# A message-passing layer in one stream of matmuls: the source-row products stand two tiles later, layer two three tiles later

## The chip, the cores and the metric

The kernel runs on one core of one Trainium2 chip. The metric is the device time of one execution in microseconds (us), the median of several runs. A core has five engines that run their own instruction streams and wait for each other by semaphores: TensorE (PE; its weight loads are shown as PEld), VectorE (DVE), ScalarE (ACT), GpSimd (POOL) and SyncE (SP, which here only issues DMAs).

## The reference

One layer of a graph network with 12500 nodes, 400000 edges sorted by `dst`, 32 features, 64 hidden units:

```python
h = jnp.maximum(_layernorm(x, axis=-1), 0.0)
# _L0_gnn_ref(h, edge_index = [src, dst], edge_attr_32, W1, b1, W2, b2):
e_feat = jnp.concatenate([h[src], h[dst], edge_attr], axis=-1)   # 400000 x 96
hid = jax.nn.relu(e_feat @ W1 + b1)
v = hid @ W2 + b2                                                # 400000 x 32
x_cand = jax.ops.segment_max(v, dst, num_segments=num_nodes)
out = x + jnp.maximum(x_cand, h)
```

## The kernel before

**Tiling.** The edges are cut into 4 stripes (`NS`), and each stripe into 196 chunks (`NCH`) of 512 edges (`C`). Four stripes of a chunk lie side by side on the 128 partitions, 32 features each. The main loop takes two chunks at a time: `for c in range(0, NCH - 4, 2)`, with `a, b = c + 2, c + 3` as the pair of chunks that the *next* iteration will need. So one iteration, called a pair below, finishes chunks c and c+1 and prepares rows for a and b. There are 98 pairs in all.

**Layer one** of a pair fills four PSUM banks `ph` (one per stripe) in three steps, 8 matmuls each: `edges_into` adds the products with the edge features (tile `ea`), `windows_into` those with the destination nodes (spans: `of` is a one-hot matrix that ACT makes, `qf` a window of already multiplied rows `q_d`), and `rows_into` those with the source rows (tile `ht`). A matmul of these steps shows as two in the profile, 16 per step. Then `relu` (ACT) makes `hid`, `second_layer` multiplies by W2 into two banks `pv`, and DVE's `scan` runs a running maximum along the sorted edges (a penalty `pb` starts a new segment). `fewest` picks the segment ends, `add_b2` (ACT) makes `sb`, and in the next pair `leave_1` transposes it on PE, `leave_2` places it with the one-hot `last`, ACT copies to `wo`, and `leave_3` adds and writes rows to `top_d` by DMAs of SP.

**Source rows** come in two ways. Twelve of sixteen groups of 128 rows per chunk are gathered by POOL (`gather`: one indirect DMA per group into tile `gh`). The other four groups per chunk, and one more in 76 of the chunks (`MMX`), are picked on PE: `tile(c, m)` multiplies one-hot matrices `hot` (DVE makes four of seven slices in `one_hots`, ACT three in `one_hots_act`) by the node table `hs`, 14 matmuls of 128x448 into one bank `pv`, and DVE multiplies by a `mask` and takes a maximum (`one`, `gm`). This is called a tile. `to_features(c, part)` transposes gathered or picked rows into `ht` (DVE); the last part, `J`, turns the picked rows.

**What sets the order.** The kernel is written under a manual schedule: each engine executes its instructions in the order in which the Python code calls them, and only the waits are added. PSUM banks `ph`, `pv` come from one ring of 7 (`bank`). POOL's gathers are paced by hand: the table `HELD` maps the position of a gather within a pair to an instruction (by pair distance and name, such as `(2, 'ea')`) that must have passed first; `passes(...)` marks these.

Of the kernel before, what the change touches and what calls it, by code (L numbers as in the profile page):

```python
# [36 lines left out]
J = C // P  # L37
# [30 lines left out]
LATE = NCH - 8  # L68
END = LATE - 16
PIECE = 2 * A0  # L70
GP = 3
HELD = {0: (3, 'b1'), 1: (3, 'b1 max'), 2: (3, 'b2'), 3: (3, 'b2 max'), 4: (3, 'b3'), 5: (3, 'b3 max'), 6: (3, 'n0'),
        8: (2, 'ea'), 9: (2, 'ht'), 10: (2, 'tr'), 12: (2, 'relu'), 13: (2, 'a1'), 14: (2, 'a1 max'), 15: (2, 'a2'),
        16: (2, 'a2 max'), 17: (2, 'a3'), 19: (2, 'lv'), 20: (2, 'scan'), 21: (2, 'b0'), 22: (2, 'b0 max')}
# [16 lines left out]
def gnn_kernel(ctx, tc, x, src, src_mm, src_x, src_t, dst, dst_end, dst_ext, lo, lo_c, ends_b, edge_attr, weights, w1, w2, b2, out):  # L91
# [501 lines left out]
    with tc.tile_pool(name="edges", bufs=3) as pool, tc.tile_pool(name="edges_ps", bufs=1, space=PSUM) as ps:  # L593
# [106 lines left out]
        def leave_1(c, sb):  # L700

            px = bank("pv")[:, :P]
            passes(c // 2 + 1, "tr", nc.tensor.transpose(px, sb, ident))  # L703
# [235 lines left out]
        for c in range(0, NCH - 4, 2):  # L939
            a, b = c + 2, c + 3  # L940
            if c:
                ph = edges_into(c)
                windows_into(c, ph)
            rows_into(c, ph)
            if c % LOAD:
                load_edges(c + LOAD // 2 + AHEAD)
# [7 lines left out]
            if c == LATE + 2:  # L954
                ea = pool.tile([P, LOAD * C], F32, name="ea", bufs=2)
                rows_of(1, slice(32, 64), [ea[:, :LOAD * C // 2], ea[:, LOAD * C // 2:]])
                for k in range(c, NCH, 2):
                    late_loads(k)
            if c:
                so = leave_1(c - 2, sb)  # L960
                one_hots(b, 0, 2)
                one_hots_act(b)
                one_hots(b, 2, by_act(b).start)
                mask_of(b)
                if c == LATE + 2:
                    finish(0)
                tile(a, 1)
                to_features(a, 1)
                leave_rest(so)
                one_hot_x(b)  # L970
                tile(a, 2)
                to_features(a, 2)
                last_next = lasts(c)
                tile(a, 3)
            else:
                tile(b, 3)
                tile(a + 2, 0)
            pv = second_layer(c, hid)
# [29 lines left out]
            if not c:  # L1008
                last_next = lasts(c)
# [80 lines left out]
        c = NCH - 4  # L1090
# [198 lines left out]
```

## Time and profile before

| | |
|---|---|
| median of 3 runs | 3555.01 us (3553.36 to 3557.04) |
| profiled execution, its own time | 3587.46 us |
| span of the profiled execution | 3585.7 us |
| mean granted TensorE clock | 0.939 |
| busy: PE, PEld | 3293.3 us (92%), 2511.2 us (70%) |
| busy: DVE, ACT, POOL | 2437.4 us (68%), 1402.3 us (39%), 2161.2 us (60%) |
| matmuls | 18468 |

The profile is one execution, so 1.8 us lie outside its span, and it is 0.9% longer than the median of the runs. Busy PE means that a matmul was in flight; its ends are modelled, and it says little of how dense the matmuls stand. The start times of successive groups in the timeline tell more. "issue" as the releaser of a wait means that the profile shows nothing that the engine waited for.

### The profile page before, as it was taken

How to read it: one execution, taken by the hardware profiler on the slowest of the kernel's cores; microseconds unless marked ns; L12 is line 12 of the kernel's file. 1: busy time of each engine (PE TensorE's matmuls, PEld its weight loads, DVE VectorE, ACT ScalarE, POOL GpSimd, SP SyncE). 2: the span in 40 equal slices, each digit the busy share in tenths (PEclk: the TensorE clock that was granted, in tenths of full speed). 3: DMA queues.
4: the chain of work that ended last, by engine and by line, in shares of the span. 5: the costliest groups of instructions: out<-in, count | busy, mean ns of one | idle time of the engine just before them, and what ended most of it. 6: DMA issues, size and time to landing. Idle time of an engine off the chain costs nothing.

```text
span 3585.7 us, 55025 instructions
## 1 busy us (share of the span) xinstructions
PE 3293.3 (92%) x18468; PEld 2511.2 (70%) x18468; DVE 2437.4 (68%) x4987; ACT 1402.3 (39%) x2276; POOL 2161.2 (60%) x2295
## 2 busy tenths in 40 slices
PE   5788999999999999999999999999999999999996
PEld 3466767776767677767776767777767777677773
DVE  6467667767677677676666666767666766666765
ACT  4233434343443333434333334333333344343342
POOL 6665666665666666656666666666666666666562
PEclk8799999999999999999999999999999999999997
DMA  5322222222222222222222222222222222221222
GB/s 188 82 60 58 58 59 58 71 50 58 68 63 52 58 65 63 52 58 62 62 56 64 62 59 56 59 63 66 50 63 63 62 53 62 61 66 50 59 58 64
DMA packets 183894, 227.88 MB, mean 64 GB/s; under 512 B 115365, under 2 KB 155445, under 8 KB 170806
## 3 DMA queue, kind: packets, MB, share of 16 engines
q10 hardware_dynamic: 36228, 109.11, 9.6%
q0 software_dynamic: 72992, 37.52, 7.7%
q1 hardware_dynamic: 74386, 77.71, 7.0%
q8 instruction: 145, 2.38, 0.3%
q14 instruction: 143, 1.17, 0.1%
HBM read 212.63 MB, written 11.47 MB: 63 GB/s over the span
## 4 chain that ended last, share of the span: by engine, by line
PE 70%; DVE 12%; issue 8%; another core or an unknown queue 4%; DMA 1%; ACT 1%; POOL 1%; SPq 1%; DVEq 0%; ACTq 0%; POOLq 0%
PE pv L351 53%; PE ph L837 12%; DVE one L358 3%; PE pv L871 3%; DVE hot L311 2%; DVE pv L878 2%; DVE ht L375 1%; PE pv L727 1%; POOL gh L186 1%; DVE sm L885 1%; PE pv L703 1%; DMA top_d<-wo 1%; DVE gm L359 1%; DVE m L892 0%
## 5 line engine op out<-in xcount | busy, mean ns | idle before, releaser
L186 POOL DMA_INDIRECT gh<-h_d,src_i x2249 | 2123.6, 944 | 1355.9 <-issue 511.8
L351 PE MATMUL pv<-hs,hot 128*128 128x448 f32 x10752 | 2369.3, 378 | 112.5 <-issue 76.7
L351 PEld LDWEIGHTS pv<-hs,hot 128*128 128x128 f32 x10752 | 2096.1, 197 | 326.8 <-issue 127.0
L358 DVE TENSOR_TENSOR one<-pv,mask 128x448 f32<-128x448 f32 x768 | 470.4, 612 | 982.7 <-issue 340.1
L862 ACT ACTIVATE hid<-ph,wt 128x512 f32<-128x512 f32 x392 | 244.2, 687 | 982.0 <-remote 491.2
L359 DVE TENSOR_REDUCE gm<-one 128x32 f32<-128x448 f32 x768 | 476.3, 620 | 26.4
L311 DVE TENSOR_TENSOR hot<-kb,consts 128x1024 fp32r<-128x1024 f16 (+1 forms) x379 | 445.4, 1194 | 0.0
L837 PE MATMUL ph<-ht,wt 32*64 32x512 f32 x1568 | 350.4, 696 | 95.0 <-issue 59.3
L325 ACT ACTIVATE hot<-away,ones 128x512 fp32r<-128x512 f32 x582 | 421.8, 725 | 36.9 <-remote 17.9
L324 ACT ACTIVATE away<-kb,key_n 128x512 f32<-128x512 f16 x582 | 415.7, 714 | 0.0
L718 ACT ACTIVATE wo<-pv 128x256 f32<-128x256 f32 x95 | 36.5, 384 | 689.7 <-remote 383.9
L837 PEld LDWEIGHTS ph<-ht,wt 32*64 32x64 f32 x1568 | 84.1, 141 | 294.3 <-issue 246.2
L878 DVE TENSOR_TENSOR_SCAN pv<-pb,kept,pv 128x512 f32<-128x512 bf16 x193 | 244.0, 1264 | 15.1 <-remote 15.0
L375 DVE STREAM_TRANSPOSE ht<-gh 128x96 f32<-128x96 f32 x774 | 207.9, 269 | 2.6
L697 ACT ACTIVATE sb<-m,wt 128x128 f32<-128x128 f32 x97 | 39.1, 403 | 423.1 <-DVE sm L885 239.4
L351 PE MATMUL pv<-hs,xg 128*128 128x448 f32 x760 | 169.2, 366 | 8.1 <-issue 8.1
L351 PEld LDWEIGHTS pv<-hs,xg 128*128 128x128 f32 x760 | 143.1, 189 | 21.4 <-issue 11.6
L837 PE MATMUL ph<-of,qf 32*64 32x512 f32 x1552 | 136.3, 606 | 14.3 <-ACT of L672 11.2
L672 ACT ACTIVATE of<-of,ones 128x512 f32<-128x512 f32 x194 | 140.6, 725 | 6.3
L892 DVE TENSOR_REDUCE m<-sm 128x64 f32<-128x512 f32 x194 | 133.1, 686 | 6.7
L671 ACT ACTIVATE of<-db,below 128x512 f32<-128x512 int32 x194 | 137.4, 708 | 0.0
L837 PE MATMUL ph<-ea,wt 32*64 32x512 f32 x1568 | 131.3, 619 | 3.7 <-issue 2.6
(139 smaller groups left out, 1309.4 us busy)
## 6 DMA issues: line engine op xcount, KB each, us to landing
ea<-in_edge_attr SPq DMA_DIRECT2D x49, 1024.0 KB
db<-in_dst_ext ACTq DMA_DIRECT2D x48, 1024.0 KB
gh<-h_d,src_i POOLq DMA_INDIRECT x2249
pb<-pen_d ACTq DMA_DIRECT2D x47, 512.5 KB
kb<-key_d ACTq DMA_DIRECT2D x47, 512.0 KB
top_d<-wo SPq DMA_DIRECT2D x752, 3.0 KB
qf<-q_d SPq DMA_DIRECT2D x392, 16.0 KB
q_d<-qs SPq DMA_DIRECT2D x6, 512.0 KB
```

Of the source, the lines that this page charges most:

```text
L186: ins = nc.gpsimd.indirect_dma_start(out=parts[-1][:, i, :], out_offset=None, in_=h_d[:, :], in_offset=bass.IndirectOffsetOnAxis(ap=src_i[ ...
L311: nc.vector.tensor_tensor(hot_of(c)[:, start:stop], keys[c][:, None, :].to_broadcast([P, n, MM * P]), key_ps[:, start:stop, None].to_broad ...
L324: nc.scalar.activation(away, keys[c], AF.Square, bias=key_n[:, k:k + 1])
L325: nc.scalar.activation(hot_of(c)[:, k], away, AF.Relu, bias=ones, scale=-1.0)
L351: ins = nc.tensor.matmul(po, hot[k], hs[:, part, k].rearrange("p f a -> p (f a)"), start=(k == 0 and part == 0), stop=(k == A1 - 1 and par ...
L358: nc.vector.tensor_tensor(one, of_group, mask[:, None, :].to_broadcast([P, D, A0]), op=ALU.mult)
L359: passes(c // 2 - 1, "ab"[c % 2] + str(m) + " max", nc.vector.tensor_reduce(row, one, axis=AX.X, op=ALU.max))
L375: nc.vector.transpose(ht[:, r].rearrange("p k e -> p (k e)"), gh[c][part][:, :r.stop - r.start].rearrange("p k f -> p (k f)"))
L672: nc.scalar.activation(of, of, AF.Relu, bias=ones, scale=-1.0)
L837: ins = nc.tensor.matmul(ph[s][x * HID:(x + 1) * HID], w[g], e[g], start=start, stop=stop)
L862: passes(c // 2, "relu", nc.scalar.activation(hid[k], of, AF.Relu, bias=b1c))
L878: ins = nc.vector.tensor_tensor_scan(pv, pen[:, :C], pv, -LOW if before is None else before, op0=ALU.add, op1=ALU.max)
```

## The change

No instruction is added or removed from the work; two or three waits apart, each engine has the same instructions in another order.

- After `edges_into` and `windows_into`, tiles (a,1) and (a,2) now come before `rows_into` and `relu`; tile (a,3) and the transpose of `leave_1` follow.
- `second_layer` and `leave_2` now stand behind tiles (a,3), (b,0) and (b,1), where they stood behind (a,1), (a,2) and (a,3).
- DVE's one-hots, masks and row transposes and ACT's one-hots for chunk a+2 move with the tiles that they belong to; `one_hots(b, ...)` now stands ahead of `relu`.
- `HELD` is written anew: which gather waits for which instruction.

```diff
-HELD = {0: (3, 'b1'), 1: (3, 'b1 max'), 2: (3, 'b2'), 3: (3, 'b2 max'), 4: (3, 'b3'), 5: (3, 'b3 max'), 6: (3, 'n0'),
...
+HELD = {0: (3, 'b2'), 2: (3, 'b2 max'), 3: (3, 'b3'), 4: (3, 'b3 max'), 7: (3, 'n0'),
...
             if c:
                 ph = edges_into(c)
                 windows_into(c, ph)
+                one_hots(b, 0, 2)
+                one_hots_act(b)
+                tile(a, 1)
+                to_features(a, 1)
+                one_hots(b, 2, by_act(b).start)
+                mask_of(b)
...
+                tile(a, 2)
+                to_features(a, 2)
             rows_into(c, ph)
...
             hid = relu(c)
...
             if c:
+                tile(a, 3)
                 so = leave_1(c - 2, sb)
-                one_hots(b, 0, 2)
-                one_hots_act(b)
-                one_hots(b, 2, by_act(b).start)
-                mask_of(b)
...
-                tile(a, 1)
-                to_features(a, 1)
+                to_features(a, 3)
+                to_features(a, J)
+                one_hot_x(b)
+                tile(b, 0)
+                to_features(b, 0)
                 leave_rest(so)
-                one_hot_x(b)
-                tile(a, 2)
-                to_features(a, 2)
+                one_hots(a + 2, 0, 2)
+                one_hots_act(a + 2)
+                tile(b, 1)
+                to_features(b, 1)
                 last_next = lasts(c)
-                tile(a, 3)
+                one_hots(a + 2, 2, by_act(a + 2).start)
+                mask_of(a + 2)
...
             pv = second_layer(c, hid)
             if c:
                 pw = leave_2(c - 2, so, last)
-            if c:
-                one_hots_act(a + 2)
...
-            if c:
-                to_features(a, 3)
-                to_features(a, J)
...
-            if c:
-                one_hots(a + 2, 0, 2)
             found, kept = scan(c, pv[0], kept)
             m8 = fewest(found, 0)
             if c:
-                tile(b, 0)
-                to_features(b, 0)
+                tile(b, 2)
+                to_features(b, 2)
             found, kept = scan(c + 1, pv[1], kept)
             sb = add_b2(fewest(found, 1, m8))
...
-            if c:
-                tile(b, 1)
-            to_features(b, 1)
...
-            if c:
-                one_hots(a + 2, 2, by_act(a + 2).start)
-                mask_of(a + 2)
             last = last_next
-            if c:
-                tile(b, 2)
-            to_features(b, 2)
```

TensorE, one pair in the steady state before (`ea`, `of`, `ht` are the three steps of layer one, `x14` of `pv<-hs,hot` is one tile, `zero` and `xg` hold the one-hots of the extra group, `ident,sb` is the transpose of `leave_1`, `hid,wt` layer two, `so,last` `leave_2`):

```order
L837 MATMUL ph<-ea,wt 64x512 x8
L837 MATMUL ph<-of,qf 64x512 x8
L837 MATMUL ph<-ht,wt 64x512 x8
L703 MATMUL pv<-ident,sb 128x128
L351 MATMUL pv<-hs,hot 128x448 x42
L871 MATMUL pv<-hid,wt 32x512 x8
L727 MATMUL pv<-so,last 128x256 x2
L351 MATMUL pv<-hs,hot 128x448 x56
```

The same pair of the changed kernel, on TensorE:

```order
L837 MATMUL ph<-ea,wt 64x512 x8
L837 MATMUL ph<-of,qf 64x512 x8
L351 MATMUL pv<-hs,hot 128x448 x28
L837 MATMUL ph<-ht,wt 64x512 x8
L351 MATMUL pv<-hs,hot 128x448 x14
L703 MATMUL pv<-ident,sb 128x128
L351 MATMUL pv<-hs,hot 128x448 x28
L871 MATMUL pv<-hid,wt 32x512 x8
L727 MATMUL pv<-so,last 128x256 x2
```

The 24 small matmuls of layer one no longer stand in one row: 16 of them, then two tiles, then the other 8. After `leave_2` follow 42 to 56 large matmuls where 70 to 84 followed.

VectorE, around layer two's scan before (`pv<-pb,kept,pv` is the scan, `one` and `gm` evaluate a tile, `hot` is a one-hot slice pair for a tile of the next pair):

```order
L378 STREAM_TRANSPOSE ht<-gm 128x128
L311 TENSOR_TENSOR hot<-kb,consts 128x1024
L878 SCALAR_TENSOR_TENSOR pv<-pb,kept,pv 128x512
L883 COPY kept<-pv 128x1
L885 SCALAR_TENSOR_TENSOR sm<-pb,pv 128x512
```

The same place of the changed kernel, on VectorE:

```order
L358 TENSOR_TENSOR one<-pv,mask 128x448
L359 TENSOR_REDUCE gm<-one 128x32
L375 STREAM_TRANSPOSE ht<-gh 128x96
L681 TENSOR_TENSOR last<-consts,at 128x256
L311 TENSOR_TENSOR hot<-kb,consts 128x1024
L330 TENSOR_TENSOR mask<-consts,place_k 128x56
L878 SCALAR_TENSOR_TENSOR pv<-pb,kept,pv 128x512
```

Ahead of the scan now stand a tile's evaluation (of (b,1)), the one-hot `last`, a `hot` slice pair and a mask, which stood elsewhere in the pair.

On ScalarE the six activations of `one_hots_act(b)` now stand between the spans' one-hots and `relu`, where they stood behind `relu`; the DMAs that load `db` and `pb` are issued behind them.

More of the change, by code (lines that the diff above doesn't have):

```diff
@@ L71 @@
 GP = 3
-HELD = {0: (3, 'b1'), 1: (3, 'b1 max'), 2: (3, 'b2'), 3: (3, 'b2 max'), 4: (3, 'b3'), 5: (3, 'b3 max'), 6: (3, 'n0'),
-        8: (2, 'ea'), 9: (2, 'ht'), 10: (2, 'tr'), 12: (2, 'relu'), 13: (2, 'a1'), 14: (2, 'a1 max'), 15: (2, 'a2'),
-        16: (2, 'a2 max'), 17: (2, 'a3'), 19: (2, 'lv'), 20: (2, 'scan'), 21: (2, 'b0'), 22: (2, 'b0 max')}
+HELD = {0: (3, 'b2'), 2: (3, 'b2 max'), 3: (3, 'b3'), 4: (3, 'b3 max'), 7: (3, 'n0'),
+        8: (2, 'ea'), 11: (2, 'a1'), 12: (2, 'a1 max'), 13: (2, 'a2'), 14: (2, 'ht'), 15: (2, 'a2 max'), 16: (2, 'relu'),
+        17: (2, 'a3'), 19: (2, 'b0'), 20: (2, 'b0 max'), 21: (2, 'b1'), 22: (2, 'lv'), 23: (2, 'scan')}
 BANKS = 7
@@ L943, in gnn_kernel @@
                 windows_into(c, ph)
+                one_hots(b, 0, 2)
[4 more added lines that the diff above has]
+                mask_of(b)
+                if c == LATE + 2:
+                    finish(0)
+                tile(a, 2)
+                to_features(a, 2)
             rows_into(c, ph)
@@ L1004, in gnn_kernel @@
                 finish(2)
-            if c:
-                tile(b, 1)
-            to_features(b, 1)
             if not c:
+                to_features(b, 1)
                 last_next = lasts(c)
-            if c:
-                one_hots(a + 2, 2, by_act(a + 2).start)
-                mask_of(a + 2)
+                to_features(b, 2)
             last = last_next
-            if c:
-                tile(b, 2)
-            to_features(b, 2)
             if c == LATE + 2:
```

2 lines of the change are left out of this document (removed).

## The prediction

> **What bounds the kernel now.** I read the engines' shares and the chain of waits first, then the costliest groups, then TensorE's timeline of single pairs, and last the clock.
>
> ```profile
> PE 3293.3 (92%) x18468; PEld 2511.2 (70%) x18468; DVE 2437.4 (68%) x4987; ACT 1402.3 (39%) x2276; POOL 2161.2 (60%) x2295
> PEclk8799999999999999999999999999999999999997
> PE 70%; DVE 12%; issue 8%; another core or an unknown queue 4%; DMA 1%; ACT 1%; POOL 1%; SPq 1%; DVEq 0%; ACTq 0%; POOLq 0%
> ```
>
> TensorE carries 70% of the chain and is in flight 92% of the span, so the question is how much of that is matmul at full pace. Layer one's three steps have the same count and nearly the same shapes, and should cost the same:
>
> ```profile
> L837 PE MATMUL ph<-ht,wt 32*64 32x512 f32 x1568 | 350.4, 696 | 95.0 <-issue 59.3
> L837 PE MATMUL ph<-of,qf 32*64 32x512 f32 x1552 | 136.3, 606 | 14.3 <-ACT of L672 11.2
> ```
>
> They don't: with the idle time ahead of it, the step with source rows takes 445.4 us and the one with spans 150.6. The timeline of one pair shows where (start, length, matmuls):
>
> ```profile
> 1674.77 1.11 PE L837 MATMUL ph<-ea,wt 32*64 32x512 f32 x16
> 1675.68 1.06 PE L837 MATMUL ph<-of,qf 32*64 32x512 f32 x16
> 1676.54 1.92 PE L837 MATMUL ph<-ht,wt 32*64 32x512 f32 x8
> 1678.80 1.36 PE L837 MATMUL ph<-ht,wt 32*64 32x512 f32 x3 [0.34 <-issue]
> 1680.32 3.38 PE L837 MATMUL ph<-ht,wt 32*64 32x512 f32 x5 [0.17 <-issue]
> 1683.63 0.47 PE L703 MATMUL pv<-ident,sb 128*128 128x128 f32 x1
> 1683.76 10.83 PE L351 MATMUL pv<-hs,hot 128*128 128x448 f32 x42
> 1694.52 1.09 PE L871 MATMUL pv<-hid,wt 64*32 64x512 f32 x16
> ...
> 1695.88 11.38 PE L351 MATMUL pv<-hs,hot 128*128 128x448 f32 x56
> ...
> 1712.78 0.69 PE L837 MATMUL ph<-ea,wt 32*64 32x512 f32 x8
> ```
>
> Edge and span products take 0.91 and 0.86 us from start to start, the source rows 7.09 us (1676.54 to 1683.63). VectorE is not what they wait for: the last transpose into `ht` was over at 1675.51, before the first of them.
>
> ```profile
> 1675.24 0.27 DVE L378 STREAM_TRANSPOSE ht<-gm 128x128 f32<-128x128 f32 x1
> 1930.69 0.27 DVE L378 STREAM_TRANSPOSE ht<-gm 128x128 f32<-128x128 f32 x1
> ```
>
> The second row belongs to another pair, where that transpose was late and TensorE had to wait for it until 1930.96, 0.84 us. There the rest came at once:
>
> ```profile
> 1930.12 0.59 PE L837 MATMUL ph<-ht,wt 32*64 32x512 f32 x1
> ...
> 1930.55 1.58 PE L837 MATMUL ph<-ht,wt 32*64 32x512 f32 x15
> 1932.06 0.33 PE L703 MATMUL pv<-ident,sb 128*128 128x128 f32 x1
> 1932.14 8.65 PE L351 MATMUL pv<-hs,hot 128*128 128x448 f32 x42
> 1940.73 1.09 PE L871 MATMUL pv<-hid,wt 64*32 64x512 f32 x16
> ...
> 1942.09 0.97 PE L351 MATMUL pv<-hs,hot 128*128 128x448 f32 x4
> ...
> 1945.39 9.80 PE L351 MATMUL pv<-hs,hot 128*128 128x448 f32 x48 [1.04 <-issue]
> ...
> 1960.78 0.69 PE L837 MATMUL ph<-ea,wt 32*64 32x512 f32 x8
> ```
>
> All sixteen pass in 1.94 us with the wait. So a wait of under a microsecond removes a stall of six. My reading: after 32 small matmuls in a row TensorE has used up the instructions that were ready, the next ones arrive one or two at a time, and a short wait, or slower large matmuls, lets them catch up. In this pair the shortage shows later and smaller, behind layer two's 16 small ones: the 84 matmuls from 1942.09 take 18.69 us, where those from 1695.88 took 16.90 (0.2 each).
>
> The stall has a second price, the clock:
>
> ```profile
> core 0: 3585.7 us, clock 0.939
> 1674.80:1683.60 8.80, 8.17 (x49) 1.97 (x48) 4.38 (x9) 0.91 (x2) 4.91 (x6) 0.89 0.41 82
> 1683.60:1712.80 29.20, 29.20 (x149) 25.84 (x149) 21.02 (x44) 13.27 (x22) 18.43 (x20) 0.92 0.24 65
> 1928.09:1960.78 32.69, 31.45 (x194) 25.03 (x193) 24.34 (x50) 14.30 (x23) 19.60 (x21) 1.00 0.20 50
> ```
>
> (Column eight is the granted clock.) The pair with the long stall runs at 0.92 behind it, and its first three tiles take 10.76 us instead of 8.59; the pair without runs at 1.00. The first takes 38.0 us, the second 32.7.
>
> [...]
>
> **The change, part by part.** The sum is made against 3587.5 us, the profiled execution's own time; the median of the runs is 3555.0, or 0.991 of it.
>
> ```profile
> L862 ACT ACTIVATE hid<-ph,wt x392: 676/687/702, 104.7 to 3567.6; 128x512 f32<-128x512 f32 x196
> ```
>
> 392 activations of four per pair are 98 pairs, so a pair takes (3567.6 - 104.7) / 97 = 35.7 us on average.
>
> *Source rows behind two tiles.* Edges and spans are then 32 small matmuls in a row, not 48, and 28 large ones (2 x 14 at 0.2 us, 5.7 us) pass before the next 16. Sixteen behind large ones are what layer two is now, and its row runs in 1.02 us. I take the source rows at the spans' price: 445.4 - 150.6 x 1568/1552 = 293 us gone.
>
> *The clock.* (1 - 0.939) x 3585.7 = 219 us of full clock are lost. The first two slices and the last stand at 8, 7 and 7 tenths; I estimate 60 us for them. Of the other 159, 70% lie behind the stall (0.08 x 29.2 = 2.3 us against 0.11 x 8.8 = 1.0 inside it, which is already counted): 111 us gone.
>
> *The shortage comes back smaller.* 32 small matmuls, now followed by tile (a,1), stand between the 16 of layer two, with 1.79 us behind them, and the 48 now, with 6. At least nothing, at most those 6 us a pair (582 in all). I take 1.8 us, since what follows is a large tile as there, in the pairs that had the long stall and hence had not this one: at 38.0 us for a long pair and 32.7 for a short one, an average of 35.7 makes 55 of 97 long, so 99 us come back. The short pairs' waits for the late transpose go, 42 x 0.84 = 35 us, since two tiles now cover it. One-hots are made earlier too, and of the 36 us that tiles waited for something named I count off 25, an estimate from the first row:
>
> ```profile
> L351 PE MATMUL pv<-hs,hot 128*128 128x448 f32 x10752 | 2369.3, 378 | 112.5 <-issue 76.7
> L186 POOL DMA_INDIRECT gh<-h_d,src_i x2249 | 2123.6, 944 | 1355.9 <-issue 511.8
> ```
>
> *Layer two later.* Behind its end now stand `leave_2` and three or four tiles instead of five or six: 0.34 + 4 x 14 x 0.2 + 0.9 = 12.5 us until the next pair's span products, 9.6 without the extra group. In that time VectorE must scan twice and ScalarE make the spans' one-hots. Prices from before, start to start:
>
> ```profile
> 1591.05 1.28 DVE L878 TENSOR_TENSOR_SCAN pv<-pb,kept,pv 128x512 f32<-128x512 bf16 x1
> ...
> 1593.76 0.61 DVE L358 TENSOR_TENSOR one<-pv,mask 128x448 f32<-128x448 f32 x1
> ...
> 1595.13 1.25 DVE L878 TENSOR_TENSOR_SCAN pv<-pb,kept,pv 128x512 f32<-128x512 bf16 x1
> ...
> 1597.81 0.41 DVE L764 TENSOR_TENSOR wo<-pv,wo 128x256 f32<-128x256 f32 x1
> 1597.92 0.40 ACT L697 ACTIVATE sb<-m,wt 128x128 f32<-128x128 f32 x1 [4.85 <-DVE sm L885]
> ...
> 1600.35 0.72 ACT L672 ACTIVATE of<-of,ones 128x512 f32<-128x512 f32 x1
> ```
>
> and, of the costliest groups:
>
> ```profile
> L311 DVE TENSOR_TENSOR hot<-kb,consts 128x1024 fp32r<-128x1024 f16 x377 | 440.9, 1188 | 0.0
> L681 DVE TENSOR_TENSOR last<-consts,at 128x256 fp32r<-128x256 f32 x96 | 37.0, 385 | 0.0
> ```
>
> Scan 2.71, a tile 1.37, scan 2.68, then 3.2 for `sb` and four activations: 10.0 us. Ahead of them VectorE has tile (b,1), 1.37 us, `last`, 0.39, and a `hot` pair, 1.19: 3 us from that tile's end, 2 of them behind layer two's end. So 12 us against 12.5: hidden in the 76 pairs with an extra group, by half a microsecond, and 2.4 us late in the other 18 of the steady state: 43 us. What waits behind is the span products and the whole of TensorE.
>
> *Banks, DMAs, gathers.* The four `ph` banks are held for two tiles longer; the ring still hands out each bank seven allocations later, and the next users (transpose, (b,0), (b,1), layer two) stand behind `relu`, so nothing. `db`, `pb` and keys are issued up to 4.3 us later (six activations), two pairs ahead of use: nothing. A gather takes 0.944 us and 0.30 to the next; 2249 over 97 pairs are 23.2 x 1.245 = 28.9 us a pair, with the holds some 30. That cover ends if TensorE gets below 30 us.
>
> The sum: 3587 - 293 - 111 + 99 - 35 - 25 + 43 = 3265, or 3.3 us less a pair. From the other side, the short pair of 32.7 less its wait is 31.8; with 30 in the 21 pairs without the group that is 31.4 on average, and 3587 - 97 x 4.3 = 3170. I take the middle, 3218; by 0.991, **3190 us**. Its own range goes from all shortage gone, with gathers the bound (3587 - 97 x 5.5 = 3054, or 3025), to 33.3 a pair (3355, or 3325).
>
> **The rivals.**
>
> *The same stall, elsewhere.* If TensorE runs dry after 32 small matmuls as after 48, tile (a,1) stalls by 6 us. Only clock, transposes and one-hots are won, and the late spans lost: 3587 - 111 - 35 - 25 + 43 = 3459, or 3430. For it: the shortage did move, to 1943. Against: there it was 1.8.
>
> *The stall travels.* If it belongs to the products with source rows themselves, they stall wherever they stand, 6 us between two tiles, and the clock still falls: no change, 3555. The pair at 1930 speaks against it. [...]
>
> *Spans too late, slower.* If VectorE comes to layer two's scan with a backlog, span products wait in every pair and give the shortage no cover that counts. The gain is (293 + 111 - 99 + 35 + 25) / 97 = 3.8 us a pair, so it decides once they wait that long in each; at 5 us a pair, 3265 - 43 + 97 x 5 = 3707, or 3675. VectorE is busy 68%, 25 of 35.7 us, which leaves room; the chain has none.
>
> *Another bound first.* Gathers and holds at 34 us a pair: 3587 - 97 x 1.7 = 3422, or 3390.
>
> **How the numbers follow.** Forecast 0.64, same stall elsewhere 0.12, another bound 0.10, stall travels 0.05, slower by late spans 0.09. The predicted time is the forecast's. The range runs from 3030 to 3430, which takes in the first three. Within 0.2% is about what a measurement of this kernel can tell from no change. Faster 0.86, same 0.05, slower 0.09.
>
> **What would show it.** The group of source-row products falls from 350 busy and 95 idle to the spans' 136 and 14; the granted clock rises from 0.939 to above 0.97; tile (a,1) begins with gaps of "issue". Idle time before the span products, released by ScalarE, would show the late chain. I am wrong if the source-row group keeps its time, or if TensorE's tiles wait longer than these products did.

## The result: 3.2% slower, with the named stall mostly gone

The changed kernel takes 3666.55 us (median of 4 runs, 3663.72 to 3670.64), the kernel before 3554.19 us (4 runs, 3546.98 to 3557.04): a ratio of 1.032, 95% interval 1.0301 to 1.0339. The forecast was 3190 us, with a range of 3030 to 3430.

The page of the profile after, in the same order as before (engines' busy time, then the chain of waits; the last line is from the view of cores):

```profile
PE 3322.4 (91%) x18468; PEld 2452.9 (67%) x18468; DVE 2431.5 (66%) x4987; ACT 1421.2 (39%) x2276; POOL 2165.0 (59%) x2295
PE 35%; DVE 28%; issue 12%; another core or an unknown queue 8%; DMA 7%; ACT 7%; POOL 2%; SPq 1%; ACTq 0%; DVEq 0%; POOLq 0%
core 0: 3663.0 us, clock 0.959
```

TensorE is in flight as long as before, at a better clock (0.939 before), but carries 35% of the chain instead of 70%. VectorE went from 12% to 28%, "issue" from 8% to 12%. So TensorE now waits for others. The groups on TensorE, first of before (those that the prediction didn't show), then of after (busy time, mean ns of one, then the idle time ahead of the group and its releasers):

```profile
L837 PE MATMUL ph<-ea,wt 32*64 32x512 f32 x1568 | 131.3, 619 | 3.7 <-issue 2.6
L871 PE MATMUL pv<-hid,wt 64*32 64x512 f32 x1568 | 126.1, 612 | 7.5 <-issue 5.7 <-ACT hid L862 1.2
L727 PE MATMUL pv<-so,last 128*128 128x256 f32 x192 | 48.5, 334 | 2.8 <-DVE so L710 2.8
```

```profile
L837 PE MATMUL ph<-ea,wt 32*64 32x512 f32 x1568 | 143.8, 617 | 16.2 <-issue 12.3 <-DVE sm L885 3.6
L837 PE MATMUL ph<-of,qf 32*64 32x512 f32 x1552 | 222.7, 694 | 64.5 <-ACT of L672 61.7 <-ACT of L671 1.4 <-issue 0.7
L837 PE MATMUL ph<-ht,wt 32*64 32x512 f32 x1568 | 189.9, 641 | 19.9 <-issue 15.5 <-DVE ht L378 1.7
L871 PE MATMUL pv<-hid,wt 64*32 64x512 f32 x1568 | 176.7, 609 | 24.9 <-issue 21.6 <-ACT hid L862 1.2
L727 PE MATMUL pv<-so,last 128*128 128x256 f32 x192 | 49.2, 338 | 79.5 <-DVE so L710 66.2 <-DVE gm L359 8.0 <-issue 4.6
L351 PE MATMUL pv<-hs,hot 128*128 128x448 f32 x10752 | 2371.5, 375 | 91.3 <-issue 82.2
```

Busy and idle together, the source rows fell from 445.4 to 209.8 us (-235.6). But the spans rose from 150.6 to 287.2 (+136.6), layer two from 133.6 to 201.6 (+68.0), `leave_2` from 51.3 to 128.7 (+77.4) and the edge features from 135.0 to 160.0 (+25.0). The large matmuls gained 19. These six rows alone come to +52; the spans of the two profiled executions differ by 77 (that of before was 0.9% longer than the median).

One pair after, from the timeline of all engines (TensorE but for one transpose, of the others only what bears on it):

```profile
1778.59 1.11 PE L837 MATMUL ph<-ea,wt 32*64 32x512 f32 x16
1779.58 1.07 PE L837 MATMUL ph<-of,qf 32*64 32x512 f32 x2
1780.17 0.72 ACT L672 ACTIVATE of<-of,ones 128x512 f32<-128x512 f32 x1
1780.95 1.11 PE L837 MATMUL ph<-of,qf 32*64 32x512 f32 x14 [0.30 <-ACT of L672]
1781.99 5.88 PE L351 MATMUL pv<-hs,hot 128*128 128x448 f32 x28
1787.79 1.38 PE L837 MATMUL ph<-ht,wt 32*64 32x512 f32 x8
1789.50 1.12 PE L837 MATMUL ph<-ht,wt 32*64 32x512 f32 x8 [0.33 <-issue]
1790.56 3.07 PE L351 MATMUL pv<-hs,hot 128*128 128x448 f32 x14
...
1793.49 6.01 PE L351 MATMUL pv<-hs,hot 128*128 128x448 f32 x28
1799.43 1.06 PE L871 MATMUL pv<-hid,wt 64*32 64x512 f32 x9
1801.24 1.09 PE L871 MATMUL pv<-hid,wt 64*32 64x512 f32 x7 [0.74 <-issue]
1801.33 0.62 DVE L358 TENSOR_TENSOR one<-pv,mask 128x448 f32<-128x448 f32 x1 [4.26 <-remote]
...
1802.71 0.25 DVE L710 TENSOR_TENSOR so<-pv,so 128x128 fp32r<-128x128 f32 x1
1803.02 0.51 PE L727 MATMUL pv<-so,last 128*128 128x256 f32 x2 [0.69 <-DVE so L710]
1803.36 5.78 PE L351 MATMUL pv<-hs,hot 128*128 128x448 f32 x28
...
1814.66 1.11 PE L837 MATMUL ph<-ea,wt 32*64 32x512 f32 x16
```

Three things are new. The span products wait for ScalarE until 1780.89 (2.41 us from their first start to the tiles, 0.86 before). Layer two takes 3.59 us to `leave_2`, 1.02 before. And tile (b,0), the first 14 of the 28 matmuls of 1793.49, was through by about 1796.6 (14 at 0.2 us, and the last one's length), yet VectorE begins to evaluate it at 1801.33, having sat idle for 4.26 us with a releaser that the profile can't name ("remote"). `so` stands behind that evaluation, and `leave_2` waits for it.

The start-to-start times, added over 97 pairs, say the same (us, my sums of the timeline's starts; "tiles" holds what passes before the next small group begins):

| | ea | spans | ht | layer two | tiles | sum |
|---|---|---|---|---|---|---|
| before | 118 | 102 | 432 | 125 | 2650 | 3472 |
| after | 191 | 240 | 199 | 275 | 2621 | 3565 |

(45 and 39 us of transposes and `leave_2` complete the sums.) The spans take over 1.8 us in 89 of the 97 pairs, before in 5. In the table layer two holds the wait of `leave_2`.

### The profile page after: what moved, and what is told of

The parts are those of the page before. It is cut to its first block, busy times and chain, and to the rows that moved or that the text cites. A ratio compares the mean times of both kernels' runs of the same rounds, so it can differ in the third digit from the quotient of the medians.

```text
span 3663.0 us, 54694 instructions
## 1 busy us (share of the span) xinstructions
PE 3322.4 (91%) x18468; PEld 2452.9 (67%) x18468; DVE 2431.5 (66%) x4987; ACT 1421.2 (39%) x2276; POOL 2165.0 (59%) x2295
## 4 chain that ended last, share of the span: by engine, by line
PE 35%; DVE 28%; issue 12%; another core or an unknown queue 8%; DMA 7%; ACT 7%; POOL 2%; SPq 1%; ACTq 0%; DVEq 0%; POOLq 0%
PE pv L351 26%; PE ph L837 7%; DVE one L358 5%; DVE hot L311 5%; DVE pv L878 5%; DMA pb<-pen_d 5%; ACT of L672 3%; DVE ht L375 3%; ACT of L671 2%; DVE sm L885 2%; POOL gh L186 2%; DVE m L892 2%; DVE xg L281 1%; DMA gh<-h_d,src_i 1%
## 5 line engine op out<-in xcount | busy, mean ns | idle before, releaser
L351 PE MATMUL pv<-hs,hot 128*128 128x448 f32 x10752 | 2371.5, 375 | 91.3 <-issue 82.2
L351 PEld LDWEIGHTS pv<-hs,hot 128*128 128x128 f32 x10752 | 2043.3, 193 | 470.1 <-issue 219.3
L358 DVE TENSOR_TENSOR one<-pv,mask 128x448 f32<-128x448 f32 x768 | 471.0, 613 | 1120.7 <-remote 494.3
L862 ACT ACTIVATE hid<-ph,wt 128x512 f32<-128x512 f32 x392 | 254.7, 689 | 662.2 <-PE ph L837 435.6
L311 DVE TENSOR_TENSOR hot<-kb,consts 128x1024 fp32r<-128x1024 f16 (+1 forms) x379 | 454.3, 1199 | 0.0
L837 PE MATMUL ph<-of,qf 32*64 32x512 f32 x1552 | 222.7, 694 | 64.5 <-ACT of L672 61.7
L837 PE MATMUL ph<-ht,wt 32*64 32x512 f32 x1568 | 189.9, 641 | 19.9 <-issue 15.5
L871 PE MATMUL pv<-hid,wt 64*32 64x512 f32 x1568 | 176.7, 609 | 24.9 <-issue 21.6
L837 PEld LDWEIGHTS ph<-of,qf 32*64 32x64 f32 x1552 | 43.4, 140 | 219.2 <-ACT of L672 202.8
L837 PE MATMUL ph<-ea,wt 32*64 32x512 f32 x1568 | 143.8, 617 | 16.2 <-issue 12.3
L727 PEld LDWEIGHTS pv<-so,last 128*128 128x128 f32 x192 | 29.2, 192 | 164.9 <-DVE so L710 128.6
```

The costliest lines, as they stand in the source:

```text
L311: nc.vector.tensor_tensor(hot_of(c)[:, start:stop], keys[c][:, None, :].to_broadcast([P, n, MM * P]), key_ps[:, start:stop, None].to_broad ...
L351: ins = nc.tensor.matmul(po, hot[k], hs[:, part, k].rearrange("p f a -> p (f a)"), start=(k == 0 and part == 0), stop=(k == A1 - 1 and par ...
L358: nc.vector.tensor_tensor(one, of_group, mask[:, None, :].to_broadcast([P, D, A0]), op=ALU.mult)
L837: ins = nc.tensor.matmul(ph[s][x * HID:(x + 1) * HID], w[g], e[g], start=start, stop=stop)
L862: passes(c // 2, "relu", nc.scalar.activation(hid[k], of, AF.Relu, bias=b1c))
```

## What the runs were to decide

The stall in the products with source rows was read as a shortage made by 48 small matmuls in a row. Two other readings were open. *A slow supply*: TensorE's instructions come at a bounded mean rate whatever the other engines do, so that any saving is taken back. *The gathers*: while GpSimd issues gathers back to back, TensorE's instructions start slowly and its signals of completion come late. In the expectations below, theory A is the slow supply and theory B the row of small matmuls; theories C and D are the gathers, where C expects relief from long pauses alone and D from a slightly longer gap between any two. For the gathers spoke the view of GpSimd in time, before and after:

```profile
1671.45 0.94 POOL L186 DMA_INDIRECT gh<-h_d,src_i  x1 [0.69 <-DVE gm L359]
...
1679.04 0.95 POOL L186 DMA_INDIRECT gh<-h_d,src_i  x1 [0.30 <-issue]
1681.99 0.94 POOL L186 DMA_INDIRECT gh<-h_d,src_i  x1 [2.00 <-PE ph L837]
```

```profile
1779.51 0.95 POOL L186 DMA_INDIRECT gh<-h_d,src_i  x1 [2.19 <-DVE gm L359]
...
1787.01 0.94 POOL L186 DMA_INDIRECT gh<-h_d,src_i  x1 [0.30 <-issue]
1789.83 0.94 POOL L186 DMA_INDIRECT gh<-h_d,src_i  x1 [1.88 <-PE ph L837]
...
1798.65 0.95 POOL L186 DMA_INDIRECT gh<-h_d,src_i  x1 [0.30 <-issue]
```

In the pair before that stalled, seven gathers run from 1671.45 to 1680, some 1.25 us from start to start with 0.3 us between them, and the source rows, from 1676.54 to 1683.63, stand in its end and the 3.6 us behind it. In the pair after, a run of seven ends at 1788, where the source rows trickle, and a run of eight at 1799.6, where layer two does and the signals are late. The new `HELD` had moved the runs along with the work.

## The experiments

All ratios are against the kernel before on the same chip (3553 to 3590 us there, but for the last two runs).

**1. TensorE alone, then beside one engine at a time.** A kernel of its own with the matmuls of a pair in the order before and after, ten pairs each; then the first order beside gathers, beside VectorE and ScalarE, beside plain transfers, and beside all of these.

```diff
+            large(28)
+            small(ph, False, True)
...
+        ins = nc.gpsimd.indirect_dma_start(out=gh[k % 8], out_offset=None, in_=x[:, :],
```

> This kernel leaves the network out and runs TensorE alone in stretches: 840 large matmuls; 640 small ones of the layer one shape; 800 narrow ones (16 columns); ten pairs in the order of the kernel before and ten in that of the changed one, none waiting for another engine; then ten pairs each beside gathers, beside VectorE and ScalarE, beside large transfers, and beside all. Theory A (instructions reach TensorE at some 92 ns each on average, 36936 of them in both kernels, whatever their order): the small and the narrow ones take 180 to 190 ns each in the long run (640 small ones 115 to 120 us), and a pair of 388 instructions takes 35 to 36 us in both orders, also alone. Theory B (the supply is faster than need, and only a long row of small products empties a reserve): small ones 27 to 54 ns each (640 in 17 to 35 us), pairs alone 30 to 32 us in both orders. If the supply is slowed by other work, pairs are near 30 us alone and near 36 us in the stretch beside that work.

The windows of these stretches (length, busy time of PE, PEld, DVE, ACT, POOL, then clock, DMA share and GB/s; the first has nine pairs in the order before, the others ten but for the last with nine):

```profile
291.30:560.70 269.40, 269.40 (x1720) 222.30 (x1719) 0.00 (x0) 0.00 (x0) 0.00 (x0) 1.00 0.00 1
560.70:862.90 302.20, 302.20 (x1911) 245.00 (x1910) 0.00 (x0) 0.00 (x0) 0.00 (x0) 1.00 0.00 1
862.90:1375.70 512.80, 386.93 (x1911) 274.97 (x1910) 0.00 (x0) 0.00 (x0) 226.60 (x240) 0.80 0.05 8
1375.70:1675.20 299.50, 299.50 (x1911) 247.00 (x1910) 250.01 (x400) 253.09 (x400) 0.00 (x0) 1.00 0.00 1
1675.20:1974.50 299.30, 299.30 (x1911) 247.00 (x1910) 0.00 (x0) 0.00 (x0) 0.00 (x0) 1.00 0.54 211
1974.50:2434.40 459.90, 336.20 (x1720) 248.20 (x1719) 224.87 (x360) 227.30 (x360) 218.11 (x216) 0.78 0.21 70
```

A pair takes 29.9 us alone in the order before, 30.2 after, 29.95 beside VectorE and ScalarE, 29.9 beside 211 GB/s of transfers, and 51.3 beside 24 gathers back to back a pair, which move 8 GB/s. Gathers alone do it. How it looks on TensorE some ten microseconds into a run, with a gather in flight or 0.30 us away from the next all the time:

```profile
976.90 1.06 PE L164 MATMUL pv<-ea,wt 64*32 64x512 f32 x7
978.74 1.30 PE L164 MATMUL pv<-ea,wt 64*32 64x512 f32 x4 [0.78 <-issue]
...
990.01 0.53 PE L147 MATMUL pv<-hs,hot 128*128 128x448 f32 x1 [2.06 <-issue]
991.41 0.53 PE L147 MATMUL pv<-hs,hot 128*128 128x448 f32 x1 [0.86 <-issue]
```

Matmuls with nothing to wait for come one at a time, over a microsecond apart. The stall is late, though, and it outlasts the gathers. The 24 of a pair take 29.7 of its 51.3 us, and one such run starts at 1069.76. Its first 11 us, then 15 to 30 us behind its start, then 36 to 48, on TensorE alone (the number of matmuls in brackets, then the clock):

```profile
1069.80:1080.80 11.00, 11.00 (x83) 1.00 0.08 12
1084.80:1099.80 15.00, 5.70 (x11) 0.53 0.09 13
1105.80:1117.80 12.00, 12.00 (x60) 0.99 0.00 0
```

For 11 us, nine gathers, TensorE keeps up: in all ten runs of this stretch it is then at most 0.6 us behind a pair without gathers (my comparison of start times). Then it nearly stops (11 matmuls in 15 us), and within 6.3 us of the last gather (the 24 of that run end at 1099.5) it is back at its pace: 60 matmuls in 12 us. As to 48 small ones in a row: alone, they take 2.76 us, 57.5 ns each, and 640 of them run at 53.7. The slow supply falls as a constant of the chip, and so does my count of small matmuls.

**2 to 4. Each half of the change alone, and more work for TensorE.** The second run moves only the source rows (with the holds `a1` to `relu` that belong to it), the third only layer two and its tiles. The fourth adds 16 narrow matmuls a pair to the kernel before, 32 instructions with their weight loads:

```diff
+                tile(a, 1)
...
+                tile(a, 2)
+                to_features(a, 2)
             rows_into(c, ph)
```

```diff
+                tile(a, 3)
                 so = leave_1(c - 2, sb)
...
+                tile(b, 0)
...
+                tile(b, 1)
...
             pv = second_layer(c, hid)
```

```diff
+        for k in range(EXTRA if c % 2 and m == 1 else 0):
+            for x in range(8):
+                nc.tensor.matmul(po[x % 2 * HID:(x % 2 + 1) * HID, :16], w1c[:D], ident[:D, :16], start=True, stop=True)
```

> The source rows' products alone stand two tiles later; layer two stays behind tile (a,3). Theory A: the time that the products with source rows lose before is lost at other places; 3530 to 3620 us, the same within 2%. Theory B: the stall at the source rows goes, 3250 to 3350 us.

> Layer two alone stands three tiles later, with the scans, transposes and spans that follow it; source rows stay behind the spans. Theory A: the supply is the same, and what is lost is what TensorE waits for spans while its reserve is full: 3570 to 3680 us. Theory B with late spans as the only cause of the loss: the long stall stays and the late spans are added, 3640 to 3800 us.

> The kernel before with 16 narrow matmuls more in each pair (32 instructions of 16 columns, ahead of tile (b,1)'s own, in its bank, overwritten by it), amid large ones. Theory A: 32 x 92 ns = 2.9 us a pair, 3800 to 3850 us. Theory B: their own time alone, 16 x 0.03 to 0.06 us, 0.5 to 1 us a pair, 3600 to 3655 us.

Rows alone: 3546.71 us, 0.9977 (0.9965 to 0.9989), too little to call a gain. Layer two alone: 3690.71, 1.0383 (1.0366 to 1.0400). More matmuls: 3594.29, 1.0117 (1.0100 to 1.0134). Against 3554.3 these are -8, +136 and +40 us. With the rows alone the stall I had named is gone and the time is not: source rows fall from 432 to 124 us start to start, while tiles rise from 2650 to 2746, layer two from 125 to 252, spans from 102 to 141. The 32 extra instructions cost 40 / 97 = 0.41 us a pair, 13 ns each, so no mean rate of supply is the bound. The stall moved to them all the same: with the idle time ahead of them they take 194.5 us, and the source rows fall from 445.4 to 234.4.

**5. How the gathers must stand to do it.** TensorE alone again, with gathers let loose by a ScalarE clock, evenly or in runs:

```diff
+    stretch([0, 2], 5)
+    stretch([0, 2, 4, 6, 8, 10, 12, 14], 20)
```

> This kernel leaves the network out: three pairs in the order of the kernel before alone, then stretches of ten such pairs, none waiting for another engine, beside gathers let go by a clock made of ScalarE's activations (0.63 us each): one per 1.58 us evenly; runs of 8 with a pause, the same mean; one per 1.9 us evenly; runs of 8 with a pause, the same mean; runs of 4, the same mean; one per 2.5 us evenly; runs of 8, the same mean. Theory C (gathers slow TensorE's supply of instructions while they run and for some microseconds after, and it recovers only in a pause): pairs near 30 us at a mean of 2.5 us, 32 to 45 us at 1.58 us, and at the same mean runs with a pause are better than an even pace (by 1 us a pair or more). If the supply depends on the number of gathers alone, run or even makes no difference; if a short gap is enough, the even pace is the better one.

The windows of eight pairs each, one gather in 1.66 us on average (1.33 and 1.86 us apart by turns), and runs of eight, 1.33 us apart, at the same mean (1.66):

```profile
136.40:376.20 239.80, 239.80 (x1529) 197.94 (x1528) 0.00 (x0) 228.35 (x362) 136.69 (x145) 1.00 0.07 11
512.20:761.30 249.10, 244.94 (x1534) 198.62 (x1533) 0.00 (x0) 237.21 (x376) 141.44 (x150) 1.00 0.07 11
```

Spread out, a pair takes 29.98 us, as with no gathers. In runs of eight it takes 31.1. The same holds at lower rates: at one in 2.65 us evenly 29.9, in runs of eight at nearly that mean 30.8; runs of four at 1.99 cost nothing (29.9). So in this run the disturbance shows with eight gathers in a row and not with four, and theory C had it the wrong way round. It is also much smaller here than with 24 in a row (31.1 us a pair against 51.3). That fits the 11 us of run 1, which a run of eight just reaches.

**6 and 7. The same two kernels with a third of the gathers.** One wide gather takes the place of three narrow ones, in before and in after. It reads the same number of bytes from another array, so the right source features are left out, and so are the holds of the narrow gathers that it replaces:

```diff
-            for i in range(min(SOME, n - k)):
-                ins = nc.gpsimd.indirect_dma_start(
-                    out=parts[-1][:, i, :], out_offset=None, in_=h_d[:, :],
...
+            m = min(SOME, n - k)
+            ins = nc.gpsimd.indirect_dma_start(
+                out=parts[-1][:, :m, :].rearrange("p k f -> p (k f)"), out_offset=None,
+                in_=ap(edge_attr, 0, [[m * D, N], [1, m * D]]),
...
+            hold(c, k, ins)
```

> The kernel before with one gather in place of three, each of rows three times as wide, from another array: the source features are not the right ones, the bytes and all else are the same. Theory C: the stall at the source rows' products goes (group near 136 busy as the spans'), the clock rises above 0.98, a pair takes 30 to 31.5 us, in all 2980 to 3180 us. If the row of 48 small products itself empties the supply, as forecast: 3450 to 3560 us.

> The changed kernel with one gather in place of three, as in the kernel beside it; the source features are not the right ones. Theory C: 2980 to 3250 us; without a shortage the change gives nothing back, and what layer two's later place costs (the wait for spans) remains: slower than the kernel beside it by 20 to 150 us. If the change does relieve a shortage of its own: faster than the kernel beside it.

Before with a third of them: 2939.62 us, 0.8263 (0.8247 to 0.8280). After: 3063.33, 0.8606 (0.8586 to 0.8626). Of the sixth run the chain, the source rows and VectorE's evaluation of a tile, and of the seventh the spans:

```profile
PE 92%; DMA 2%; DVE 2%; ACT 1%; issue 1%; POOL 1%; SPq 1%; ACTq 0%; POOLq 0%; DVEq 0%
L838 PE MATMUL ph<-ht,wt 32*64 32x512 f32 x1568 | 121.4, 605 | 8.5 <-DVE ht L379 8.5
L359 DVE TENSOR_TENSOR one<-pv,mask 128x448 f32<-128x448 f32 x768 | 471.1, 613 | 364.0 <-PE pv L352 222.6 <-issue 138.4 <-remote 1.3
```

```profile
L838 PE MATMUL ph<-of,qf 32*64 32x512 f32 x1552 | 152.6, 639 | 41.8 <-ACT of L673 40.6 <-issue 1.2
```

48 small matmuls still stand in one row, and the source rows take 129.9 us with their idle time instead of 445.4. The clock is 0.988. The chain is TensorE's by 92%. "remote" ahead of VectorE's evaluation, 325.2 us before and 494.3 after, is 1.3. (Run 1's gathers read an input array as well, so the other array isn't what makes the difference.) So 48 in a row do not stall by themselves; the two thirds of the gathers cost 618 us (3557.62 on this chip less 2939.62), more than the forecast hoped to gain by the order. And the change is still 124 us slower with the shortage out of the way: it costs something by itself.

**8. The changed kernel with the spans' one-hots made earlier.** ScalarE makes them ahead of the first scan, so that they no longer stand behind `sb`:

```diff
+            if c and c < NCH - 12:
+                for k in range(a, a + 2):
+                    window_hots(k)
             found, kept = scan(c, pv[0], kept)
```

> The changed kernel with the spans' activations put ahead of the first scan on ScalarE, so that they no longer stand behind sb. If the wait for spans is the loss (62 us of matmul and 203 us of weight load idle behind ScalarE, 1.5 us a pair): 3500 to 3560 us. By theory C TensorE gains the wait and loses part of the time in which instructions caught up: 3560 to 3640 us. If the spans' wait is beside the point: 3640 to 3680 us.

3657.91 us, 1.028 (1.0259 to 1.0301), beside 1.032 for the changed kernel. The wait for the spans goes (64.5 us idle to 16.7), and the time stays: idle time of the large matmuls goes from 91.3 to 199.5 us, and the clock falls to 0.936. That is the third of the cases expected. Beside the gathers the 47.8 us cured at the spans came back as 108.2 at the large matmuls.

**9 to 11. A pause of one small memset after each gather**, in before, in the rows-alone kernel and in after:

```diff
+                if (k + i) % EVERY == EVERY - 1:
+                    nc.gpsimd.memset(filler, 0.0)
```

> The kernel before with a memset of 128x1 on GpSimd (0.1 us, by the rows of its start) behind every gather: a run of gathers goes at some 1.35 to 1.45 us each in place of 1.245, and the pauses between runs get shorter. Theory D (gathers back to back delay TensorE's instructions and its done signals, and a slightly longer gap between any two lets them through): starved time and late signals fall by half or more, 3300 to 3480 us, bounded by gathers at 23.2 x 1.4 = 32.5 us a pair. If long pauses are what helps, not gaps: the same or slower, 3540 to 3700 us.

> The source rows' products alone two tiles later, with the same memset behind every gather. Theory D: 3300 to 3480 us, within 1% of the kernel before with it. If long pauses help and not gaps: 3530 to 3700 us.

> The changed kernel with the same memset behind every gather. Theory D: faster than the changed kernel by 100 us or more (3666 to below 3570), but slower than the kernel before with it by the 60 to 130 us that layer two's later place costs without any shortage. If long pauses help and not gaps: 3650 to 3800 us.

3588.21 us, 1.0001 (0.9989 to 1.0013); 3570.51, 0.9944 (0.9927 to 0.9962); 3704.33, 1.0318 (1.0295 to 1.0340). The memset takes 0.113 us (median) and fits into the 0.30 us that lie between two gathers anyhow: the pace stays at 1.25 us, and the runs tell nothing of a pause.

**12. The kernel before without holds.** Nothing on TensorE is moved:

```diff
-HELD = {0: (3, 'b1'), 1: (3, 'b1 max'), 2: (3, 'b2'), 3: (3, 'b2 max'), 4: (3, 'b3'), 5: (3, 'b3 max'), 6: (3, 'n0'),
...
+HELD = {}
```

> The kernel before without its holds: a gather goes as soon as its buffer is free. Theory D: runs get longer than 8, TensorE starves more and its done signals come later, 3600 to 4000 us. If the row of small products were the cause, holds would not matter to TensorE: 3540 to 3570 us.

4225.94 us, 1.1766 (1.1746 to 1.1786). The gathers now come in runs of up to 12, and the old stall grows; the granted clock is 0.859:

```profile
L835 PE MATMUL ph<-ht,wt 32*64 32x512 f32 x1568 | 678.6, 880 | 289.6 <-issue 257.6 <-DVE ht L376 17.3 <-DVE mask L328 3.2
```

968.2 us instead of 445.4, with every engine's order unchanged but for the times at which gathers start. With runs 6 and 12 the cause of the old stall is shown from both sides: fewer gathers take the stall away, longer runs of them double it.

**13 to 15. The change's own cost, with a third of the gathers.** The edits of runs 2 and 3, and the whole change with the spans' one-hots of run 8, each on top of that of run 6:

> The source rows' products alone two tiles later, with one gather in place of three (the source features are not the right ones): no shortage is left, so what shows is what the place itself costs. The kernel before with a third of the gathers took 2940 us, the changed one 3063. If the 124 us are the switch from small to large products that the new place adds (0.3 to 0.6 us a pair): 2970 to 3000 us. If they all belong to layer two's place: 2935 to 2960 us. Wherever relu's four activations now outlast tile (a,3): 0.3 to 0.8 us a pair more, up to 3060 us.

> Layer two alone three tiles later, with one gather in place of three (the source features are not the right ones). If the late spans are the other part of the 124 us: 2980 to 3060 us, with TensorE's waits behind the spans' activation of ScalarE. If layer two's place costs only by way of late signals: 2935 to 2960 us.

> The changed kernel with a third of the gathers and the spans' activations ahead of the first scan (the source features are not the right ones). If the late spans are what layer two's place costs without a shortage: 3063 less 40 to 75 us, 2985 to 3025 us. If not: 3050 to 3075 us.

2964.15 us, 0.8338 (0.8324 to 0.8352); 3043.07, 0.8562 (0.8547 to 0.8576); 2985.52, 0.8404 (0.8390 to 0.8418). Against run 6 the rows cost 24.5 us and layer two 103.5, together 128 for the 124 of run 7. The rows' part fits one more change between small and large matmuls in a pair: 24.5 / 97 = 0.25 us, near what the new order costs in run 1 (30.2 against 29.9). That it is this change and nothing else isn't shown. With the spans' one-hots made earlier 78 us of the 124 go (3063.33 - 2985.52), so the late spans are most of layer two's part.

**16 to 18. A longer pause.** Two memsets after each gather, then one of 128 and one of 256 elements in a row:

```diff
+                for j in range(2):
+                    nc.gpsimd.memset(filler, 0.0)
```

```diff
+    filler = const.tile([P, 128], F32, name="filler")
...
+                    nc.gpsimd.memset(filler, 0.0)
```

> The kernel before with two memsets of 128x1 behind every gather: one of them fitted into the 0.30 us that lie between two gathers anyway, two should set the pace of a run at 1.36 to 1.45 us. If a wider gap lets TensorE's instructions through: 3300 to 3500 us, starved time less than half. If only the mean pace or long pauses count: 3530 to 3640 us.

> The kernel before with one memset of 128x128 behind every gather (0.205 us by the row of its start, where 0.113 fitted into the gap): a run goes at 1.32 to 1.36 us a gather in place of 1.25, the floor by gathers is 23.2 x 1.34 = 31.1 us a pair. If a gap of 0.4 us is enough for TensorE's signals and instructions: late signals below a third of the 390 us of before, 3150 to 3400 us. If it takes the 0.9 us of the kernel with two memsets: 3500 to 3620 us.

> The same with one memset of 128x256 (some 0.3 us): 1.42 to 1.47 us a gather, floor by gathers 33.6 us a pair, 97 x 33.6 + 115 = 3370 us. If a gap of 0.5 us is enough: 3370 to 3480 us, late signals below a third of the 390 us of before, TensorE waiting for gathers. If not: 3520 to 3700 us.

Two memsets: 4111.18 us, 1.1571 (1.1548 to 1.1595). The second one stretches a gather's period to 1.83 us, so gathers become the bound (23.2 x 1.83 = 42.4 us a pair; 41.6 measured). The source rows wait for their data, and VectorE no longer for late signals:

```profile
L361 DVE TENSOR_TENSOR one<-pv,mask 128x448 f32<-128x448 f32 x768 | 465.9, 607 | 92.2 <-PE pv L354 62.6 <-issue 15.8 <-remote 9.9
L840 PE MATMUL ph<-ht,wt 32*64 32x512 f32 x1568 | 271.9, 905 | 450.1 <-DVE ht L381 371.3 <-issue 45.9 <-DVE ht L378 18.4
```

The last two runs fell on another chip, on which the kernel before itself takes 2938.38 us (7 runs, 2936.54 to 2941.78): what it takes elsewhere with a third of the gathers. There 128 elements cost 1.0492 (1.0474 to 1.0509; 3083.20 us) and 256 cost 1.1315 (1.1296 to 1.1334; 3324.79 us). Both are the pace of the gathers: 1.336 us each by 23.2 makes 31.0 us a pair (31.0 measured), 1.443 makes 33.5 (33.5 measured). The 128-element run makes nearly all its gathers in one unbroken row, and in its trace VectorE begins a tile's evaluation 0.04 us after the tile's last matmul by the records. So on that chip the disturbance isn't there to be cured, and the question whether a pause of 0.1 or 0.2 us would cure it on the others stays open.

## Why the prediction was wrong, step by step

*What stalls the source rows.* This step failed. "After 32 small matmuls in a row TensorE has used up the instructions that were ready" was argued from two pairs of one trace. In one the third group of 16 stalled; in the other a short wait came first, and it didn't. I took the wait for the cure. The same windows of time hold GpSimd's rows: in the stalling pair a run of seven gathers ends at 1680, within the stall. In the other pair the run ended at 1927.75, and a pause stood ahead of the products:

```profile
1926.80 0.95 POOL L186 DMA_INDIRECT gh<-h_d,src_i  x1 [0.30 <-issue]
1930.04 0.94 POOL L186 DMA_INDIRECT gh<-h_d,src_i  x1 [2.29 <-PE pv L351]
```

For 2.29 us no gather was issued. The smaller shortage that the prediction saw at 1943 in that pair stands at the end of a run of eight (1934.65 to 1944.33). I did read the gathers, but only as a floor of 28.9 us a pair; that they disturb TensorE was no rival. Runs 1, 6 and 12 put the stall on them: 51.3 us a pair instead of 29.9 beside gathers alone, and for the source rows 129.9 us with a third of the gathers and 968.2 with longer runs, where 445.4 stood.

*Source rows, -293 us.* -235.6 by the groups. The place was right and the size near. But it was no gain: run 2 takes 308 us away there by itself (432 to 124, start to start), and the time falls by 8.

*The clock, -111.* (1 - 0.959) x 3663.0 = 150 us of full clock are lost, 219 before: -69. I had asked for more than 0.97. The sum charged no clock for the shorter waits that come back, and in the pair shown above they cost none: against the 0.86 us of an unstalled step it loses 1.55 us at the spans and 1.9 at the source rows, and it ran at 1.00 (column eight).

```profile
1778.59:1814.66 36.07, 34.02 (x194) 25.64 (x193) 24.62 (x50) 14.47 (x24) 21.75 (x23) 1.00 0.27 73
```

*The shortage comes back, +99.* Mis-sized, and in the wrong places. It was priced behind layer two, ahead of its large matmuls. It came back ahead of and within layer two (+68.0), in the edge features (+25.0), and on the other side of the signals, as VectorE's late start: where VectorE idled ahead of a tile's evaluation (from 400 to 3300 us of the span), 1.46 us of that on average lay behind the tile's last matmul by the records before (267 cases, 390 us), and 3.11 us in the changed kernel (223 cases, 693 us). With a third of the gathers it is 0.04 us. The prediction had no term for signals. Its largest effect is `leave_2`, +77.4: `so` stands behind the evaluation of tile (b,0) on VectorE now, and TensorE behind `so`. Without the disturbance that group waits 6.8 us (run 7), so it is not the new place alone.

*Transposes -35, one-hots -25.* About right: the source rows' wait for the last transpose (25.6 of the 95.0 us of idle time before) fell to 1.7, and of the large matmuls' idle time the part with a named releaser fell from 35.8 to 9.1, though run 8 shows how little such a term holds by itself.

*Late spans, +43.* The sum of 12 us against 12.5 was right in kind and too kind in size: half a microsecond of room in 76 pairs is gone beside the gathers, and the spans are late in 89 of 97 pairs. With a third of the gathers they are late in 33, and all that hangs on them costs 78 us. In the disturbed kernel the wait itself is 61.7 us of idle time.

*Not in the sum:* what the source rows' new place costs by itself, 24.5 us (run 13).

*Gathers as a floor.* Right as a rate: where a pause stretches the gathers, a pair takes exactly 23.2 of them (31.0 us at 1.336 each in run 17, 33.5 at 1.443 in run 18). And 2939 us, where nothing else disturbs, is 29.4 us a pair.

*The rivals.* "Slower by late spans" has the sign, and with 3675 us nearly the time; but its mechanism, spans that wait 3.8 us in each pair, isn't what happened. They take 1.4 us a pair more ((240 - 102) / 97), and the rest is that the gain of 3.8 us a pair never came. "The same stall, elsewhere" describes the rows alone best (run 2), with the gathers for its cause: it made no gain to speak of, 0.23%. "The stall travels" for the products themselves is refuted by run 6.

*Late instructions?* The trace of run 1 has a queue that it names "instruction" (q8): 107 packets, 1.75 MB, beside 27536 matmuls and weight loads. Around the run of gathers that starts at 914.9 one of these packets comes by 920 and none from there to 963, while TensorE nearly stops and then picks up again. So that stall ended without one; what the packets hold is not shown.

What stays open: which part of a gather delays TensorE (plain transfers of 211 GB/s don't: 29.9 us a pair), why in run 1 it takes 11 us to set in and up to 6.3 to pass, and why one chip has none of it.

## What to carry to other kernels

Before work is moved away from a stall, lay the other engines' rows of the same microseconds beside it, also those of engines that nothing waits for; a stall with "issue" as its releaser has no owner in the profile, and the order of instructions isn't the only suspect. Thin out the suspect (fewer gathers, the same everything else) before building on a reading of two pairs: one run of it would have shown 48 small matmuls in a row without the stall (129.9 us at the source rows, where 445.4 stood). Look for a consumer that idles on "remote" although its producer's last record is old: VectorE did so here for 494.3 us ahead of its evaluations (1.3 in run 6). Work behind such a consumer shouldn't be put on the path: `leave_2` took 77.4 us more there.

## What the runs showed of the hardware

In run 1 indirect gathers of GpSimd back to back (0.94 us each, 0.30 between) slow TensorE, which shares no data with them: a pair's matmuls take 51.3 us instead of 29.9, and the granted clock falls to 0.80. With nothing else going on there, the first 11 us of a run cost at most 0.6 us, and TensorE is back at its pace within 6.3 us of the last gather. Spread out at 1.66 us on average they cost nothing in run 5 (29.98 us a pair). In this kernel two thirds of them are worth 618 us of 3558 (run 6), and letting them run without holds costs 636 (run 12). It depends on the chip: one of those used ran the kernel before in 2938.38 us, the others in 3553 to 3590. A memset of 0.113 us after each gather is free (ratio 1.0001 in run 9); a second costs 0.6 us of the gathers' period (1.25 to 1.83 us, run 16).

Of the versions run that leave all of the work in, the rows alone were the only one below the kernel before by more than the noise, by 0.23% (and 0.56% with the memset, on another chip).
